# A selective-scan block with a quantised layer on one core: the quantised product formed transposed, its bias added by TensorE, and x1's statistics and x*D moved to ScalarE

## The chip, the cores and the metric

One core of one Trainium2 chip runs the whole kernel. The metric is the device time of one execution in microseconds (us). The kernel before took 2896.49 us (median of three runs, 2894.33 to 2896.74). The profile is of a further execution, which took 2897.0 us, of which 2895.2 us are the profiled span; the working of the prediction starts from that execution.

The five engines are called TensorE (PE in the profile; its weight loads are PEld), VectorE (DVE), ScalarE (ACT), GpSimd (POOL) and SyncE (SP, which issues most transfers). Each takes its instructions in the order in which the program lists them for it.

## The reference

x is 8 x 2048 tokens of 512 channels, float32. Cut to what matters:

```python
def layernorm(x):                     # over the 512 channels
    return (x - mean(x)) / sqrt(var(x) + 1e-5)

u     = layernorm(x)
xp    = u @ x_proj.T                  # 64 + 16 + 16 columns: d_rank, B, C
delta = softplus(d_rank @ dt_proj.T + dt_b)
# per channel d and state n (16 of them), over the 2048 tokens of a batch row:
h[t]  = exp(delta[t] * A) * h[t-1] + delta[t] * B[t] * u[t]
y[t]  = sum_n h[t] * C[t] + u[t] * D
x1    = x + y

z     = layernorm(x1)
scale = max(max|z|, 1e-6) / 127       # one per token
q     = clip(round(z / scale), -128, 127)
out   = x1 + (q @ wq.T) * scale * w_scale + bias
```

## The kernel before

**Tiling.** The 16,384 tokens are cut into 32 chunks of 512 (`k`). A chunk has four channel tiles of 128 (`d`) and 16 states, that is 64 scans of 128 channels x 512 tokens. One scan is one VectorE instruction (`scan`, L828). The program is written out as a sequence of 64 **slots** to a chunk, one scan each (L1105 to L1128). Four slots make a group `s`: two states by two channel tiles. Groups 0 to 7 of a chunk are channel pair `dp` 0 (slots 0 to 31), groups 8 to 15 are `dp` 1 (slots 32 to 63).

**What a scan needs.** ScalarE makes its factor exp(delta*A) (`exp_unit`, L766, tile `da`, three buffers of a group each). TensorE makes its second input delta*B*u in PSUM (`b_pe`, L813, tile `pb`, two buffers): one call of 8 products, recorded as 16 matmuls, serves two scans, and is issued at every even slot `u` for scans `u+2` and `u+3`. So the products of slot `u` can't start before scan `u-1` has freed their buffer. GpSimd multiplies each finished group with C (`c_mult`, L855) and, except in the first chunk of a batch row, writes the carried first column of `da` (`carry`, L780). TensorE then turns the products back and adds them up in PSUM (`y_pe`, L888, tile `y`, one buffer): 16 transposes 10 slots and 16 more 12 slots after the group's first slot.

**Beside the scans** two stages are spread over the slots by tables (L27 to L82). `prep(k)` makes the next chunk ready: statistics (L248, L252), normalisation (L310), four turned tiles (L322, L328), `xp` (L334, L344), four products `pdt` (L365), four softplus (L375), and four products delta*u (`dlt_pe` L288, `du` L388). `post(k)` runs one chunk later and finishes a chunk: `residual` copies x1 out of PSUM (L619), statistics of x1 on VectorE, `norm` (L633), `amax` (L652), `scales` and `inverses`, `add_bias` on GpSimd (L645), `rnd` (L670), four transposes each in `q_pe` (L675), `q_act` (L681), `o_pe` (L692), `o_out` (L701, VectorE) and `add_x1` on GpSimd (L713). The last two chunks use `LATE_AT`.

**What sets the order.** `keep_in_program_order` pins every instruction, so the tables are the order. In a slot the exps come first, then `b_pe` and the scan, then what the tables put there. Exps run ahead of the scans by up to 11 (L96, L1116 to L1119), but none is issued in the slots of `EXP_NONE`, around the softplus, because exp and softplus take a table load (ACT_TABLE_LOAD) at each change between them. The tiles of `misc` (L283, two PSUM buffers) are used in turn by `pxn`, `pxp`, `pbt`, `pdt`, `pdl`, `pz` and `po`.

**Start.** `prep_first` prepares chunk 0; `zero_diagonals` and `store_diagonals` (L214, L268) fill a table in DRAM from which `load_dg` (L799) fetches the diagonal matrices of B. All those transfers are in SP's queue.

Of the kernel before, what the change touches and what calls it, by code (L numbers as in the profile page):

```python
# [17 lines left out]
P = 128  # L18
# [10 lines left out]
    aggregate=(-49, -49, -44, -39),  # L29
    rstd=-37,  # L30
    norm=(-1, 0, 1, 2),
    xnt_pe=(4, 4, 8, 8),
    xnt_act=(6, 6, 10, 10),
    xp_pe=(10, 12, 16, 18),
    xp_act=20,
    bt_pe=22,
    bt_act=23,
    dt_pe=(24, 26, 30, 32),
    softplus=(27, 28, 32, 34),
    carry_mul=36,  # L40
    carry_exp=44,
    dlt_pe=(38, 38, 42, 42),
    du=(40, 41, 43, 44),
# [3 lines left out]
    residual=(9, 10),  # L47
    stats=(13, 16, 18, 22),
    aggregate=(19, 21, 24, 25),
    rstd=26,  # L50
    norm=(35, 36, 37, 38),
    amax=(38, 41),
    scales=42,
    inverses=45,
    add_bias=(40, 44),
    rnd=(46, 47, 48, 49),
    q_pe=(50, 50, 58, 60),
    q_act=(52, 53, 60, 62),
    o_pe=(54, 56, 62, 64),
    o_out=(56, 58, 64, 66),  # L60
    add_x1=(60, 68),
    store=(66, 74),
# [3 lines left out]
    residual=(9, 10),  # L66
    stats=(14, 18, 20, 20),
    aggregate=(18, 19, 20, 21),
    rstd=21,
    norm=(24, 25, 27, 30),  # L70
    amax=(28, 31),
    scales=32,
    inverses=34,
    add_bias=(33, 36),
    rnd=(37, 39, 39, 43),
    q_pe=(38, 42, 46, 50),
    q_act=(41, 43, 47, 51),
    o_pe=(44, 48, 52, 54),
    o_out=(46, 50, 54, 56),
    add_x1=(55, 60),  # L80
    store=(60, 64),
# [5 lines left out]
REUSED = 3  # L87
LOAD_AT = (18, 20)
SKIP_AT = ((20, 20, 22, 28), (48, 48, 52, 52))
ADD_X_AT = ((34, 36), (66, 70))  # L90
LAST_ADD_X_AT = (58, 60)
FIRST_HALF_AT = (41, 42)
Y_AT = (10, 12)
Y_FIRST_AT = (12, 14)
EXP_NONE = (27, 28, 29, 30, 31, 32, 33)
# [4 lines left out]
def kernel(  # L100
# [38 lines left out]
    bcp = ctx.enter_context(tc.tile_pool(name="bc", bufs=5))  # L139
# [48 lines left out]
    pin(nc.sync.dma_start(out=dsk_sb, in_=d_skip.rearrange("(c p) -> p c", p=P)))  # L188
    for k in range(1, min(3, NCHUNK)):
        load_x(k)  # L190
    wq_i32 = work.tile([P, ND, OUT // 4], I32, tag="hc", bufs=3, name="wq_i32")
    pin(nc.sync.dma_start(out=wq_i32, in_=wq_t.rearrange("(c p) o -> p c o", p=P)))
    zeros = work.tile([P, T], F32, tag="hc", bufs=3, name="zeros")
    pin(nc.vector.memset(zeros, 0.0))
# [5 lines left out]
    diag_d = const.tile([P, ND, P], F32, name="diag_d")  # L200
    wq_sb = const.tile([P, ND, OUT], BF16, name="wq_sb")
    ws_b = const.tile([P, OUT], F32, name="ws_b")
    bias_b = const.tile([P, OUT], F32, name="bias_b")
# [22 lines left out]
    def gpsimd_constants():  # L226

        for d in range(ND):
            pin(
                nc.gpsimd.tensor_scalar(  # L230
                    diag_d[:, d, :], ident, dsk_sb[:, d : d + 1], None, ALU.mult
                )
            )
        pin(nc.gpsimd.tensor_copy(wq_sb, wq_i32.bitcast(I8)))

# [5 lines left out]
    mvs, nmrs, rstds, x1, zs, qts = {}, {}, {}, {}, {}, {}  # L241
    das, pbs, dgs, hs, hcs, ys = {}, {}, {}, {}, {}, {}

    def stats(key, i, src):
        if key not in mvs:
            mvs[key] = small.tile([P, 2 * NT, 2], F32, tag="mv", bufs=2, name=f"mv_{key}")
        st = small.tile([P, 6], F32, tag="st", name=f"st_{key}_{i}")
        pin(nc.vector.bn_stats(st, src))  # L248
        sts[key, i] = st
# [4 lines left out]
    def rstd_of(key, first, n):  # L254

        mv = mvs.pop(key)[:, ds(first, n), :]
        ve = small.tile([P, n], F32, tag="ve", name=f"ve_{key}")
        pin(nc.gpsimd.tensor_scalar(ve, mv[:, :, 1], LN_EPS, None, ALU.add))
        rstd = small.tile([P, n], F32, tag="rstd", name=f"rstd_{key}")
        pin(nc.gpsimd.tensor_tensor(rstd, ve, nhalf[:, :n], ALU.pow))  # L260
        nm = small.tile([P, n], F32, tag="nm", name=f"nm_{key}")
        pin(nc.gpsimd.tensor_scalar(nm, mv[:, :, 0], -1.0, None, ALU.mult))
        nmr = small.tile([P, n], F32, tag="nmr", name=f"nmr_{key}")
        pin(nc.gpsimd.tensor_tensor(nmr, nm, rstd, ALU.mult))  # L264
        for i in range(n):
            nmrs[key, first + i], rstds[key, first + i] = nmr[:, i : i + 1], rstd[:, i : i + 1]
# [35 lines left out]
    def prep(k):  # L302
# [98 lines left out]
        def carry_exp():  # L401
# [4 lines left out]
            stats=lambda i: stats(key, NT + i, xn[k][:, i, :]),  # L406
            aggregate=lambda i: aggregate(key, NT + i),
# [7 lines left out]
            du=du,  # L415
        )
# [4 lines left out]
        if k in (1, 2):  # L421
            once["rstd"] = lambda: rstd_of(key, NT, NT)
# [8 lines left out]
    def prep_first(second):  # L431
# [161 lines left out]
        pin(nc.sync.dma_start(out=ws_b, in_=w_scale.partition_broadcast(P)))  # L593
        pin(nc.sync.dma_start(out=bias_b, in_=bias.partition_broadcast(P)))
# [22 lines left out]
    def residual(k, dp, half):  # L617
        t = x1[k].rearrange("p i (d h c) -> p i d h c", h=2, c=HALF)[:, :, ds(2 * dp, 2), half, :]
        pin(nc.scalar.copy(t, ys[k, dp][:, half, :, :, :]))  # L619

    def post(k):
# [7 lines left out]
        def norm(i):  # L629
            if i == 0:  # L630
                zs[k] = work.tile([P, NT, DM], F32, tag="z", bufs=1, name=f"z_{k}")
            pin(
                nc.scalar.activation(  # L633
                    zs[k][:, i, :],
                    x1_of(i),
                    AF.Identity,
                    bias=nmrs.pop((key, i)),
                    scale=rstds.pop((key, i)),
                )
            )  # L640

        def add_bias(j):
            t = x1[k][:, ds(2 * j, 2), :]
            b = bias_b.unsqueeze(1).to_broadcast([P, 2, OUT])
            pin(nc.gpsimd.tensor_tensor(t, t, b, ALU.add))  # L645

        def amax(j):
            if j == 0:
                st["am"] = small.tile([P, NT], F32, tag="am", name=f"am_{k}")
            two = slice(2 * j, 2 * j + 2)  # L650
            pin(
                nc.vector.tensor_reduce(  # L652
                    st["am"][:, two], zs[k][:, two, :], AX.X, ALU.max, apply_absolute_value=True
                )
            )
# [11 lines left out]
        def rnd(i):  # L667

            z = zs[k][:, i, :]
            pin(nc.scalar.activation(z, z, AF.Copy, bias=ROUND, scale=st["rs"][:, i : i + 1]))  # L670

        def q_pe(i):
            pz = misc(f"pz_{k}_{i}")
            for d in range(ND):
                pin(nc.tensor.transpose(pz[:, ts(d, P)], zs[k][:, i, ts(d, P)], ident))  # L675
            st["pz", i] = pz

        def q_act(i):
            qt = work.tile([P, ND, P], BF16, tag="qT", name=f"qT_{k}_{i}")
            pin(  # L680
                nc.scalar.activation(  # L681
                    qt, st.pop(("pz", i)).rearrange("p (d t) -> p d t", t=P), AF.Copy, bias=-ROUND
                )
            )
            qts[i] = qt

        def o_pe(i):
            po = misc(f"po_{k}_{i}")
            qt = qts.pop(i)
            for d in range(ND):  # L690
                pin(
                    nc.tensor.matmul(  # L692
                        po, lhsT=qt[:, d, :], rhs=wq_sb[:, d, :], start=(d == 0), stop=(d == ND - 1)
                    )
                )
            st["po", i] = po

        def o_out(i):

            pin(  # L700
                nc.vector.scalar_tensor_tensor(  # L701
                    zs[k][:, i, :],
                    st.pop(("po", i)),
                    st["xs"][:, i : i + 1],
                    ws_b,
                    ALU.mult,
                    ALU.mult,
                )
            )

        def add_x1(j):
            o = zs[k][:, ds(2 * j, 2), :]
            pin(nc.gpsimd.tensor_tensor(o, o, x1[k][:, ds(2 * j, 2), :], ALU.add))  # L713

        def store(j):
# [3 lines left out]
                    in_=zs[k][:, ds(2 * j, 2), :],  # L719
# [6 lines left out]
            residual=lambda half: residual(k, DP - 1, half),  # L726
            stats=lambda i: stats(key, i, x1_of(i)),
            aggregate=lambda i: aggregate(key, i),
# [4 lines left out]
            o_pe=o_pe,  # L733
            o_out=o_out,
        )
        pair = dict(amax=amax, add_bias=add_bias, add_x1=add_x1, store=store)
        n = 2 * NT if k + 3 < NCHUNK else NT
        once = dict(rstd=lambda: rstd_of(key, 0, n), scales=scales, inverses=inverses)
# [160 lines left out]
    def skip_pe(k, dp, i):  # L899

        for d2 in range(2):
            d = 2 * dp + d2
            for half in range(2):
# [5 lines left out]
                        rhs=diag_d[rows, d, rows],  # L909
# [5 lines left out]

    def finish():


        k, s = NCHUNK - 1, LAST - 1
        dp, np_ = place(s)[1:]  # L920
# [77 lines left out]
        def turned(i):  # L998
            qt = work.tile([P, ND, P], BF16, tag="qT", name=f"qT_last_{i}")
# [79 lines left out]
    for s in range(LAST - 1):  # L1079
        for part in range(2):  # L1080
            at = (Y_AT if s % NPAIR else Y_FIRST_AT)[part]
            plan(4 * s, [(at, lambda s=s, part=part: y_pe(s, part))])
    for k in range(NCHUNK):
        plan(k * SLOTS, [(LOAD_AT[j], lambda k=k, j=j: load_x1(k, j)) for j in range(2)])
        for dp in range(DP):
# [6 lines left out]
        plan(  # L1092
            k * SLOTS,
            [(FIRST_HALF_AT[h], lambda k=k, h=h: residual(k, 0, h)) for h in range(2)],
        )
# [82 lines left out]
```

## Time and profile before

| | us |
|---|---|
| three runs | 2894.33, 2896.49, 2896.74 |
| the profiled execution | 2897.0 |
| its span | 2895.2 |
| DVE busy, share | 2714.7, 94% |
| POOL busy, share | 2762.3, 95% |
| PE busy, share | 2577.8, 89% |
| ACT busy, share | 2061.6, 71% |
| bn statistics (L248) 244 times, 672 ns each | 158.8 |
| add_bias (L645) 62 times, add_x1 (L713) 62 times | 146.5, 147.3 |

How to read it: a group's line has the line of the kernel, the engine, the operation, output <- inputs, their sizes and the count; then busy time in all and the mean of one in ns; then the idle time of that engine just before these instructions and what ended most of it. The mean of one includes the part that overlaps with the next instruction: two scans in a row take 2.33, six 6.85, so one more scan costs 1.12 or so. A busy share is a mean over all stages. In the waits view a line says which instruction waited for which, the total in us, how many times, and the longest.

### The profile page before, as it was taken

How to read it: one execution, taken by the hardware profiler on the slowest of the kernel's cores; microseconds unless marked ns; L12 is line 12 of the kernel's file. 1: busy time of each engine (PE TensorE's matmuls, PEld its weight loads, DVE VectorE, ACT ScalarE, POOL GpSimd, SP SyncE). 2: the span in 40 equal slices, each digit the busy share in tenths (PEclk: the TensorE clock that was granted, in tenths of full speed). 3: DMA queues.
4: the chain of work that ended last, by engine and by line, in shares of the span. 5: the costliest groups of instructions: out<-in, count | busy, mean ns of one | idle time of the engine just before them, and what ended most of it. 6: DMA issues, size and time to landing. Idle time of an engine off the chain costs nothing.

```text
span 2895.2 us, 89048 instructions
## 1 busy us (share of the span) xinstructions
PE 2577.8 (89%) x37880; PEld 2077.8 (72%) x37880; DVE 2714.7 (94%) x2950; ACT 2061.6 (71%) x3550; POOL 2762.3 (95%) x1238
## 2 busy tenths in 40 slices
PE   7888998988988889989899998999998998998977
PEld 6777776766776777777777777777777777776766
DVE  5999999999999999999999999999999999999998
ACT  5777767777677776777776786767777767777764
POOL 4999999999999999999999999999999999999998
PEclk8999999999999999999999999999999999999998
DMA  6545455455554555554555445555545555555551
GB/s 199 148 126 155 162 162 171 132 139 164 166 165 137 140 155 166 157 165 131 144 165 167 162 142 139 155 165 157 158 137 147 166 166 163 143 137 154 145 168 63
DMA packets 298091, 440.24 MB, mean 152 GB/s; under 512 B 150944, under 2 KB 151456, under 8 KB 293728
## 3 DMA queue, kind: packets, MB, share of 16 engines
q1 hardware_dynamic: 296640, 434.32, 50.9%
q8 instruction: 300, 4.92, 0.7%
q14 instruction: 95, 0.78, 0.1%
q10 hardware_dynamic: 1056, 0.23, 0.0%
HBM read 394.63 MB, written 39.85 MB: 150 GB/s over the span
## 4 chain that ended last, share of the span: by engine, by line
DVE 42%; PE 30%; ACT 14%; issue 8%; DMA 4%; POOL 2%; SPq 0%; DVEq 0%; ACTq 0%; POOLq 0%
DVE h L828 34%; PE pb L813 13%; ACT da L766 6%; PE y L888 6%; PE y L906 3%; PE pdt L365 3%; ACT L766 3%; DMA dg<-dg 3%; DVE st L248 3%; DVE z L701 2%; POOL hc L855 2%; DVE x L388 1%; ACT z L633 1%; ACT L375 1%; DVE am L652 1%
## 5 line engine op out<-in xcount | busy, mean ns | idle before, releaser
L828 DVE TENSOR_TENSOR_SCAN h<-da,pb 128x512 f32<-128x512 f32 x2048 | 2348.5, 1200 | 85.4 <-PE pb L813 44.0
L855 POOL TENSOR_TENSOR hc<-h,c 128x2048 f32<-128x2048 f32 x511 | 2320.9, 4548 | 41.9 <-DVE h L828 21.7
L766 ACT ACTIVATE da<-delta,a_neg 128x511 f32<-128x511 f32 (+1 forms) x2048 | 1332.6, 712 | 529.3 <-DVE h L828 294.9
L813 PEld LDWEIGHTS pb<-dg,x 64*128 64x128 f32 x16384 | 1037.3, 192 | 697.1 <-issue 606.3
L813 PE MATMUL pb<-dg,x 64*128 64x128 f32 x16384 | 1218.6, 289 | 293.8 <-DVE h L828 143.4
L888 PE MATMUL y<-ident,hc 64*128 64x64 f32 x16352 | 688.9, 224 | 9.5 <-POOL hc L855 4.9
L888 PEld LDWEIGHTS y<-ident,hc 64*128 64x128 f32 x16352 | 658.4, 141 | 13.7 <-POOL hc L855 6.5
L375 ACT ACTIVATE delta<-pdt,dtb_sb 128x512 f32<-128x512 f32 x124 | 85.2, 687 | 157.0 <-PE pdt L365 156.3
L248 DVE BATCH_NORM_STATS2 st<-x 128x6 f32<-128x512 f32 x244 | 158.8, 672 | 0.0
L713 POOL TENSOR_TENSOR z<-z,x 128x1024 f32<-128x1024 f32 x62 | 147.3, 2376 | 0.0
L645 POOL TENSOR_TENSOR x<-x,bias_b 128x1024 f32<-128x1024 f32 x62 | 146.5, 2362 | 0.1
L601 PE MATMUL y<-x,ident 128*128 128x512 f32 x256 | 144.8, 648 | 0.0
L906 PE MATMUL y<-diag_d,xnT 64*128 64x64 f32 x2048 | 143.6, 272 | 0.0
L365 PE MATMUL pdt<-xp,dtproj_sb 128*128 128x512 f32 x248 | 140.5, 649 | 0.0
L334 PE MATMUL pxp<-xnT,xproj_sb 128*96 128x512 f32 x248 | 137.2, 635 | 0.0
L906 PEld LDWEIGHTS y<-diag_d,xnT 64*128 64x128 f32 x2048 | 130.8, 189 | 0.8 <-issue 0.8
L652 DVE TENSOR_REDUCE am<-z 128x2 f32<-128x1024 f32 x62 | 74.8, 1207 | 60.2 <-ACT z L633 60.2
L692 PE MATMUL po<-wq_sb,qT 128*128 128x512 bf16 x496 | 128.6, 382 | 0.0
L780 POOL TENSOR_TENSOR da<-first_a,state 128x4 f32<-128x4 f32 x384 | 82.6, 215 | 40.6 <-DVE h L828 35.6
L670 ACT ACTIVATE z<-z,rs 128x512 f32<-128x512 f32 x124 | 85.4, 712 | 24.7 <-DVE rs L664 24.7
L633 ACT ACTIVATE z<-x,nmr,rstd 128x512 f32<-128x512 f32 x124 | 99.0, 800 | 3.5 <-POOL nmr L264 3.5
L310 ACT ACTIVATE x<-x,nmr,rstd 128x512 f32<-128x512 f32 x120 | 95.6, 804 | 0.0
(108 smaller groups left out, 1523.8 us busy)
## 6 DMA issues: line engine op xcount, KB each, us to landing
c<-bc SPq DMA_DIRECT2D x416, 512.0 KB, 4.4
dg<-dg SPq DMA_DIRECT2D x413, 256.0 KB, 4.8
x<-in_x_dram SPq DMA_DIRECT2D x64, 512.0 KB, 6.3
x<-in_x_dram SPq DMA_DIRECT2D x31, 1024.0 KB, 6.3
out_dram<-z SPq DMA_DIRECT2D x62, 512.0 KB, 3.2
dg<-zeros SPq DMA_DIRECT2D x16, 256.0 KB, 6.6
x<-in_x_dram SPq DMA_DIRECT2D x4, 256.0 KB, 4.6
bc<-xp SPq DMA_DIRECT2D x32, 32.0 KB, 1.6
```

Of the source, the lines that this page charges most:

```text
L248: pin(nc.vector.bn_stats(st, src))
L334: nc.tensor.matmul(st["pp"][:E], lhsT=xproj_sb[:, d, :], rhs=xn_t[k][:, d, :], start=(d == 0), stop=(d == ND - 1),)
L365: nc.tensor.matmul(pd, lhsT=dtproj_sb[:, ts(d, P)], rhs=xp, start=True, stop=True)
L601: nc.tensor.matmul(ys[k, dp][:, half, :, :, :], lhsT=ident, rhs=t, start=False, stop=False, skip_group_check=True,)
L645: pin(nc.gpsimd.tensor_tensor(t, t, b, ALU.add))
L713: pin(nc.gpsimd.tensor_tensor(o, o, x1[k][:, ds(2 * j, 2), :], ALU.add))
L766: nc.scalar.activation(das[s][:, n2, d2, own], delta[k][:, d, own], AF.Exp, scale=a_neg[:, d, n : n + 1])
L813: nc.tensor.matmul(pb[:, h, :, i, :], lhsT=xn[k][rows, i, ts(d, P)], rhs=dgs[k, np_][rows, i, :, :], start=True, stop=True,)
L828: nc.vector.tensor_tensor_scan(hs[s][:, n2, d2, :], das[s][:, n2, d2, :], pbs[u // 2].rearrange("p h q i n -> p (h q i) n")[:, :, n2], 0.0 ...
L855: nc.gpsimd.tensor_tensor(hc, h, c.unsqueeze(2).to_broadcast([P, 2, 2, T]), ALU.mult)
L888: nc.tensor.matmul(ys[k, dp][:, half, i, d2, :], lhsT=hc[rows, ts(i, P)], rhs=ident[rows, rows], is_transpose=True, start=first, stop=last ...
L906: nc.tensor.matmul(ys[k, dp][:, half, i, d2, :], lhsT=xn_t[k][rows, d, ts(i, P)], rhs=diag_d[rows, d, rows], start=False, stop=False, skip ...
```

## The change

`post` and what surrounds it are rebuilt:

- x1 leaves PSUM by `y_out`, four ScalarE instructions of 256 columns for each `dp`, which also sum each token's row. GpSimd adds the two sums. Four ScalarE `square` instructions give the variance. VectorE's `stats` and `aggregate` of x1 go; those of x stay.
- After `y_out` has read `y`, TensorE adds the bias into the same PSUM tile (`bias_pe`, two bf16 matmuls with three rows, the bias split into three bf16 parts). `xb_act` then copies x1 + bias into a tile `xb`. `add_bias` and `add_x1` on GpSimd go.
- `norm` and `rnd` work in place on x1. `o_pe` has the weights stationary and all 512 tokens moving, so the product comes out with channels on partitions; `u_act` scales it by w_scale (one per partition) on ScalarE; `ut_pe` turns it back with four transposes per 128 tokens; `o_out` multiplies by the token's scale and adds `xb` in one VectorE instruction.
- x*D is multiplied by ScalarE in place (`skip_act`, once `xp` has been made), and `skip_pe` becomes plain transposes.
- Slots move. `dt_pe` goes from (24, 26, 30, 32) to (26, 28, 32, 34), the softplus from (27, 28, 32, 34) to (28, 29, 33, 35), `EXP_NONE` from 27-33 to 28-34, `amax` from (38, 41) to (28, 30), `rnd` from 46-49 to 37-40, `q_pe` from (50, 50, 58, 60) to (42, 42, 50, 50). `y`'s first transposes go from slots 12 and 14 of a `dp` to slot 14.
- `bc` has 4 buffers where it had 5, and 2 groups of a chunk where it was 3 reuse the C and diagonals of the first half.
- At the start GpSimd splits the bias (three casts, two copies, two subtractions, one partition of 512) where it made `diag_d`; the three transfers of the parts stand in SP's queue ahead of `zero_diagonals(0)`. The two broadcasts of w_scale and bias go from there to slot 20 of the last chunk.

```diff
 PREP_AT = dict(
-    dt_pe=(24, 26, 30, 32),
-    softplus=(27, 28, 32, 34),
+    dt_pe=(26, 28, 32, 34),
+    softplus=(28, 29, 33, 35),
+    skip_act=(30, 30, 31, 31),
-    dlt_pe=(38, 38, 42, 42),
-    du=(40, 41, 43, 44),
+    dlt_pe=(40, 40, 44, 44),
+    du=(42, 43, 45, 46),
...
 POST_AT = dict(
+    sums=11,
+    squares=(14, 15, 16, 17),
+    rstd=22,
+    norm=(25, 26, 26, 27),
+    amax=(28, 30),
+    scales=31,
+    inverses=36,
+    rnd=(37, 38, 39, 40),
+    q_pe=(42, 42, 50, 50),
+    q_act=(44, 45, 52, 53),
+    o_pe=(54, 56, 58, 60),
+    u_act=(56, 58, 60, 62),
+    ut_pe=(64, 64, 66, 66),
+    o_out=(66, 67, 68, 69),
+    store=(72, 76),
...
-FIRST_HALF_AT = (41, 42)
+Y_OUT_AT = ((41, 41, 42, 42), (73, 73, 74, 74))
+BIAS_AT = (43, 75)
+XB_AT = ((44, 45), (76, 77))
-Y_FIRST_AT = (12, 14)
+Y_FIRST_AT = (14, 14)
-EXP_NONE = (27, 28, 29, 30, 31, 32, 33)
+EXP_NONE = (28, 29, 30, 31, 32, 33, 34)
...
+    def y_out(k, dp, i):
+            nc.scalar.activation(
+                x1[k][:, i, ds(dp * 2 * P, 2 * P)].rearrange(...),
+                ys[k, dp][:, :, i, :, :].rearrange("p h d c -> p d h c"),
+                AF.Identity,
+                accum_out=x1[k, "s"][:, dp, i : i + 1],
...
+    def bias_pe(k, dp):
+        for half in range(2):
+                nc.tensor.matmul(
+                    ys[k, dp][:, half, :, :, :],
+                    lhsT=ones_3,
+                    rhs=row[:, :, half, :].unsqueeze(1).to_broadcast([3, NT, 2, HALF]),
+                    start=False, stop=False, skip_group_check=True,
...
+    def skip_act(k, d):
+        t = xn_t[k][:, d, :]
+        pin(nc.scalar.activation(t, t, AF.Copy, scale=dsk_sb[:, d : d + 1]))
```

The two queues of the changed kernel, as built, between slots 24 and 50 of a chunk ("wait" names what the built program waits for there):

```
ScalarE: exp 32,33; xp; exp 34,35; norm x1 0; BT; state; norm 1,2,3; table load;
  softplus 0,1; state; skip_act x4; softplus 2; state; table load; exp 36,37;
  table load; softplus 3; table load; exp 38,39; exp 40,41; rnd 0; state; exp 42,43;
  rnd 1; exp 44,45; rnd 2; exp 46,47; rnd 3; exp 48,49; y_out x2; state; exp 50,51;
  y_out x2; exp 52,53; q_act 0; xb 0; exp 54,55; q_act 1; xb 1; ...
TensorE: slot 32: b_pe (wait: scan 31), y x16, pdt 2; slot 34: b_pe, y x16, pdt 3; ...
  slot 42: b_pe, pz 0, pz 1, bias x2 (wait: the fourth y_out);
  slot 44: b_pe for scans 46, 47; pdl 2 (wait: q_act 0); pdl 3 (wait: du 2);
  slot 46: b_pe for scans 48, 49; y of the next dp (wait: xb 1); ...
VectorE: ...; scan 44; scan 45; du 2; scan 46; du 3; scan 47; ...
```

## The prediction

> **What bounds the kernel now.** I began with the costliest groups of the page, to see which engine has least air.
>
> ```profile
> L828 DVE TENSOR_TENSOR_SCAN h<-da,pb 128x512 f32<-128x512 f32 x2048 | 2348.5, 1200 | 85.4 <-PE pb L813 44.0
> L855 POOL TENSOR_TENSOR hc<-h,c 128x2048 f32<-128x2048 f32 x511 | 2320.9, 4548 | 41.9 <-DVE h L828 21.7
> ```
>
> VectorE and GpSimd are both about 95% busy, so the shares don't say who leads. The waits of VectorE between the first and the last amax (182 to 2820 us) do:
>
> ```profile
> DVE am L652 <- ACT z L633: 60.2, 31, 2.2
> DVE h L828 <- ACT da L766: 32.6, 26, 1.3
> DVE h L828 <- PE pb L813: 27.7, 44, 2.5
> DVE h L828 <- POOL hc L855: 2.3, 3, 1.0
> ```
>
> VectorE hardly waits for GpSimd: 2.3 us in 30 chunks. It waits for ScalarE and TensorE. So VectorE leads: a chunk's amax waits end at 1421.04 and 1773.54, four chunks apart, 88.1 us each. Of that VectorE's work is 64 scans of 1.12, 8 statistics of 0.59, 8 aggregates of 0.07, two amax of 1.11, four du of 0.60, four o_out of 0.65, together 84.3 (starts of neighbours on its timeline). The other 3.8 are waits, all in one place. VectorE's timeline there:
>
> ```profile
> 1407.04 6.85 DVE L828 TENSOR_TENSOR_SCAN h<-da,pb 128x512 f32<-128x512 f32 x6 [0.29 <-PE pb L813]
> 1414.23 2.33 DVE L828 TENSOR_TENSOR_SCAN h<-da,pb 128x512 f32<-128x512 f32 x2 [0.34 <-PE pb L813]
> 1417.79 1.22 DVE L828 TENSOR_TENSOR_SCAN h<-da,pb 128x512 f32<-128x512 f32 x1 [1.23 <-ACT da L766]
> 1421.04 1.22 DVE L652 TENSOR_REDUCE am<-z 128x2 f32<-128x1024 f32 x1 [2.03 <-ACT z L633]
> ```
>
> These are scans 30-35, 36-37, 38 and the first amax. ScalarE's timeline at the same time shows why:
>
> ```profile
> 1410.39 0.69 ACT L375 ACTIVATE delta<-pdt,dtb_sb 128x512 f32<-128x512 f32 x1 [3.83 <-PE pdt L365]
> 1411.10 1.28 ACT L766 ACT_TABLE_LOAD   x1
> 1412.39 1.33 ACT L766 ACTIVATE da<-delta,a_neg 128x511 f32<-128x511 f32 x2
> 1413.74 1.28 ACT L375 ACT_TABLE_LOAD   x1
> 1415.04 0.69 ACT L375 ACTIVATE delta<-pdt,dtb_sb 128x512 f32<-128x512 f32 x1
> 1415.74 1.28 ACT L766 ACT_TABLE_LOAD   x1
> 1417.04 1.33 ACT L766 ACTIVATE da<-delta,a_neg 128x511 f32<-128x511 f32 x2
> ...
> 1428.44 1.04 ACT L619 COPY x<-y 128x512 f32<-128x512 f32 x2
> ```
>
> From the third softplus, which waits for TensorE, ScalarE works without a gap; scan 38 starts as soon as its exp is there. The windows view confirms it for 1410.39 to 1429.48, with its columns PE, PEld, DVE, ACT, POOL:
>
> ```profile
> 1410.39:1429.48 19.09, 15.81 (x198) 12.79 (x198) 15.50 (x16) 19.00 (x27) 16.10 (x8) 0.91 0.21 64
> ```
>
> ScalarE is busy 19.00 of 19.09 us, in the stage where the change adds most to it.
>
> **The sum, part by part.**
>
> *VectorE loses* four statistics and four aggregates of x1: 4 x 0.59 + 4 x 0.07 = 2.65 a chunk; 81.65 of work stay. o_out is one instruction as before (another second input; 0.65).
>
> *GpSimd loses* four instructions of 2.35 and gains about 0.7 of small ones. I count both at nothing: by the waits, VectorE doesn't wait for it. *TensorE* loses half the passes of x*D (L906's 16 in 0.89 become transposes like L888's 16 in 0.49) and gains 16 transposes (8 in 1.02, L675) and four bias matmuls: even in sum, but moved.
>
> *First stall.* The third product pdt is now at slot 32 behind the `b_pe` that waits for scan 31, so it can't be earlier than the end of scan 31. Its chain stands in the trace before one pdt earlier (1403.05 to 1405.87): wait 0.07, `b_pe` 1.16, y 0.49, pdt 1.05, then softplus; 2.85. From the softplus to scan 38 the trace has 1410.39 to 1417.79, 7.4; a state copy (0.1) is added between. So scan 38 starts 10.35 after scan 31 has ended; six scans and the reciprocal need 6.8. **3.55 lost**, where before 3.8 were lost between the late exps and amax. Amax itself no longer waits: by its slots 28 and 30 its two norms are done (rstd ends 7.8 after scan 19, two norms and BT 1.7 more: 9.5; VectorE gets there at 10.1). The four `skip_act` (0.61 each, as L670) fall into ScalarE's wait for pdt 2, about 2.1 long after them.
>
> Three table loads stand in that chain, 1.29 each from start to start. The Trainium skill (ScalarE: Activation LUTs, "What ACT_TABLE_LOAD costs") gives about 2.66 us for a switch with its drain; by that the chain, and the stall, would be 4.1 longer, which the row of before excludes.
>
> *Second stall*, the step on which the forecast rests. Count from the start of scan 38. ScalarE then issues, in its built order, 13 exps, four `rnd`, two state copies, four `y_out`. Before, from 1417.79 to 1428.44, it did 13 exps and four norms of 0.70 in 10.65. With `rnd` at 0.61: -0.36; copies +0.2; `y_out` 4 x 0.40 = 1.6. The fourth `y_out` ends at 12.1. (The trace has no `y_out`. Nearest below: the last chunk's copy of the same size, L1031, four in 1.2, 0.30 each; above: that and another small ScalarE instruction for the sum, 0.19 as L866, and some slack, 0.60. I take 0.40, near the row of equal size.) Before, only y's first transposes at slot 44 waited for this copy, after the `b_pe` of their slot. Now the bias waits for it on TensorE, and behind it stand `b_pe` for scans 46-47, pdl 2, pdl 3, `b_pe` for 48-49.
> - Bias: two bf16 matmuls, 0.49 (L692: four in 0.98; from half that to the two passes of L601, 1.05). `b_pe` 1.1: at 13.8.
> - pdl 2 waits for q_act 0 as well, two exps and 0.58 later: 12.1 + 1.8 = 13.9; transposes 0.6; VectorE's du 2 at 14.7 to 15.35.
> - pdl 3 waits for du 2; `b_pe` for 48-49 ends at 17.2. Scan 46 from 15.35, du 3, scan 47; scan 48 at 18.2.
> - Needed: ten scans and four du, 13.6. **4.6 lost** (3.8 to 6 by the bounds).
>
> *Third*: four pairs of slots in a row (54 to 60) now have `b_pe`, y and po on TensorE: 2.55 each (1444.86 to 1447.41) against 2.24 for two scans, in a stretch from which o_out has gone; 1.25 less a lead of about 0.6: **0.7 lost** (0 to 1.2).
>
> *Other additions*, counted at nothing: `square`, `u_act`, `xb_act` (0.71, 0.5, 0.5, after L633, L681, L619) lie in slots where ScalarE had slack (44.78 us busy of the 68.88 from 1429.48 to 1498.36, in the windows view). If that cover went, they would cost their 7 us. The same bias order at slot 11 leaves about 0.1 before scan 14; each 0.1 on `y_out` there costs up to 0.4. One more C and one more diagonal load a chunk: the diagonals of group 15 stand on SP behind a C load that waits for group 11's `c_mult`; by 4.8 to land they come 0.5 ahead of need; about 1 if not.
>
> A chunk: 81.65 + 3.55 + 4.6 + 0.7 = 90.5 against 88.1: **+2.4**, times 30 full chunks = 72. First chunk, with neither rounding nor q_act: both stalls smaller, +3.5. Last chunk: statistics only, -2.65. Start: SP's zero fills, issued at 26.72 before, stand behind bias parts that GpSimd has only after 29.9 and seven small instructions, 3.3 to 8.9 (a quarter of L234's cast to L1053's 1.27, each seven times); 6.5 to 12 later, two broadcasts fewer; scan 12 waited for these fills' successors (9.32): +6. Sum: +79, on the profiled 2897.0, that is 2976; the median of the runs is 0.5 lower: **2975**.
>
> The Trainium skill (Perfetto Trace Analysis, "Optimizing Scalar/DVE Operations") says that offloading to ScalarE may make sense where VectorE is saturated. By the shares of the page (94% and 71%) it holds, and would give 31 x 2.65 = 82 us; by ScalarE's 19.00 of 19.09 in this stage it doesn't.
>
> **The rivals.**
> - *VectorE keeps what it saves* (faster). Work falls by 2.65 and the old waits stay: 2897 - 82 + 6 = 2821. It is decided at slot 43: du 2 is wanted 10.2 after scan 38, and needs the fourth `y_out` at 7.6. For: the averages. Against: 13 exps alone take 8.0. Chance 0.09.
> - *GpSimd was the limit* and its 9.4 go straight to the time, down to VectorE's 81.65 a chunk: 2897 - 31 x 6.45 + 6 = 2703. For: 95% busy. Against: 2.3 us of waits. 0.03.
> - *The change moves work but the loss only balances it*: the second stall 2.2, not 4.6; 2903. Needs ScalarE some 2.4 ahead of my count. 0.05.
> - *More is late*: `y_out` at 0.60 also delays slot 12 (+0.8 twice), TensorE's run 1.2, the diagonals 1: +2.3 a chunk more, 3045. 0.11.
>
> **How the numbers follow.** The forecast has 0.72: 2975, its own range 2925 to 3020. A difference under 0.2% (6 us) can't be told from none. Faster is the first two rivals, 0.12; same 0.05; slower 0.83. The range runs from 2905, the balance, to 3030, part of the last rival; it leaves out about 0.17.
>
> **What would show it.** In the profile after: VectorE's wait for `pb` and for pdl once a chunk, some 4.6 together, about 15 us after the third softplus; TensorE idle before the bias until a `y_out`; waits for `da` twice, 1.2 and 2.3; no wait before amax; GpSimd well under 90%. The forecast is wrong if `b_pe` at slot 44 isn't late, or if the two `da` waits are gone.

## The result, and the profile after

The changed kernel takes 3011.36 us (median of four runs, 3009.24 to 3013.56), the kernel before 2896.61 beside it: ratio 1.0397, 95% interval 1.0379 to 1.0415. It is slower by 115 us; 2975 was forecast, 79 more. Its profiled span is 3009.0, 113.8 more than before.

The groups of the page of the changed kernel, which answer to those shown of before (the scan is now L913, GpSimd's product L940):

```profile
L913 DVE TENSOR_TENSOR_SCAN h<-da,pb 128x512 f32<-128x512 f32 x2048 | 2351.6, 1200 | 172.4 <-ACT da L851 109.1
L940 POOL TENSOR_TENSOR hc<-h,c 128x2048 f32<-128x2048 f32 x511 | 2320.6, 4546 | 157.2 <-PE y L973 64.4
L413 DVE TENSOR_TENSOR x<-pdl,x 128x512 f32<-128x512 f32 x124 | 84.2, 679 | 159.6 <-PE pdl L313 157.8
L658 PE MATMUL y<-bias,ones 3*128 3x512 bf16 x124 | 38.0, 386 | 91.7 <-ACT x L646 91.7
```

The scans cost what they did; the idle time ahead of them doubled (85.4 to 172.4), and du (L413), which did not wait before, has 159.6 of idle time ahead of it, 157.8 of that for the transposes pdl (`dlt_pe`). The bias on TensorE (L658) waits 91.7 for ScalarE's y_out (L646). GpSimd is 83% busy and waits too. VectorE's waits in the same stretch as before, 182 to 2820 us:

```profile
DVE x L413 <- PE pdl L313: 150.2, 44, 6.0
DVE h L913 <- ACT da L851: 101.9, 58, 2.2
DVE h L913 <- PE pb L898: 32.3, 98, 1.2
DVE h L913 <- POOL da L865: 3.0, 8, 0.4
```

The waits of amax are gone, as forecast. In their place stand du's wait, once a chunk, and the exps', twice a chunk (58 in 29 chunks). VectorE's timeline has them all in one stretch of a chunk (scan 36, scan 38 and on, du 0, du 2, scan 48):

```profile
1563.26 1.22 DVE L913 TENSOR_TENSOR_SCAN h<-da,pb 128x512 f32<-128x512 f32 x1 [1.33 <-ACT da L851]
...
1567.85 5.89 DVE L913 TENSOR_TENSOR_SCAN h<-da,pb 128x512 f32<-128x512 f32 x5 [2.20 <-ACT da L851]
1574.16 0.69 DVE L413 TENSOR_TENSOR x<-pdl,x 128x512 f32<-128x512 f32 x1 [0.42 <-PE pdl L313]
...
1583.49 0.69 DVE L413 TENSOR_TENSOR x<-pdl,x 128x512 f32<-128x512 f32 x1 [4.70 <-PE pdl L313]
...
1587.53 2.33 DVE L913 TENSOR_TENSOR_SCAN h<-da,pb 128x512 f32<-128x512 f32 x2 [0.30 <-PE pb L898]
```

From scan 38 at 1567.85 to du 2 at 1583.49 are 15.6 us, where 10.2 would do (eight scans of 1.12 and two du of 0.60). ScalarE's timeline (third softplus, the exps from 38 on, the second half of the fourth y_out, q_act 0) and its busy time from that softplus to the end of y_out, with the columns as before, show the queue behind it:

```profile
1560.38 0.69 ACT L400 ACTIVATE delta<-pdt,dtb_sb 128x512 f32<-128x512 f32 x1 [2.39 <-PE pdt L390]
...
1567.10 2.56 ACT L851 ACTIVATE da<-delta,a_neg 128x512 f32<-128x512 f32 x4
...
1579.67 0.20 ACT L646 ACTIVATION_READ_ACCUMULATOR x<-y 128x1 f32 x1
...
1580.99 0.59 ACT L752 ACTIVATE qT<-pz 128x512 bf16<-128x512 f32 x1
```

```profile
1560.38:1579.76 19.38, 14.54 (x166) 11.26 (x167) 14.36 (x15) 19.30 (x36) 15.64 (x5) 0.91 0.37 122
```

ScalarE is busy 19.30 of 19.38 us, and the exp behind the last y_out starts 11.9 after scan 38 did; for the end of y_out 12.1 was forecast. TensorE's timeline then shows what waits for it, and something that was not forecast:

```profile
1574.53 1.16 PE L898 MATMUL pb<-dg,x 64*128 64x128 f32 x16
...
1579.92 0.59 PE L658 MATMUL y<-bias,ones 3*128 3x512 bf16 x2 [2.59 <-ACT x L646]
1580.44 1.96 PE L898 MATMUL pb<-dg,x 64*128 64x128 f32 x16
1582.33 1.13 PE L313 MATMUL pdl<-ident,delta 128*128 128x128 f32 x4
...
1585.30 2.08 PE L898 MATMUL pb<-dg,x 64*128 64x128 f32 x16
```

The same 16 products of b_pe take 1.16 before the wait for y_out and 1.96 and 2.08 after it. The windows view, cut at the trace's own changes of the granted clock (the column after the five engines; 1.00 is full speed), shows with what it goes together:

```profile
1566.96:1570.37 3.41, 1.54 (x19) 0.68 (x15) 2.52 (x3) 3.40 (x8) 0.96 (x3) 1.00 0.43 141
1570.37:1573.78 3.41, 3.41 (x35) 3.29 (x36) 3.26 (x3) 3.41 (x6) 3.41 (x1) 0.50 0.27 97
...
1580.61:1587.44 6.83, 6.04 (x46) 5.09 (x48) 3.63 (x4) 4.05 (x10) 0.12 (x1) 0.50 0.39 115
```

In this chunk, after a stretch in which TensorE was busy 1.54 of 3.41 us, its clock is 0.50 for the next 3.41; after the wait for y_out it is 0.50 for another 6.83, just when everything late is queued on TensorE. That the clock is what costs there is tested below, by filling the wait.

**Where the 113.8 us are**, taken from the starts of the scans in the two traces: the start and chunk 0 +4.9, chunks 1 to 30 +117.3, the last chunk and the end -8.4. A chunk is from here on the mean of chunks 2 to 29, first scan to first scan:

| us a chunk | before | forecast for after | after |
|---|---|---|---|
| VectorE's work and gaps under 0.15 | 84.4 | 81.65 | 82.5 |
| waits at scans 36 and 38 (first stall) | 1.7 | 3.55 | 3.5 |
| wait of amax | 2.0 | 0 | 0 |
| waits from du 0 to scan 50 (second stall) | 0 | 4.6 | 5.7 |
| other waits | 0.4 | 0.7 | 0.7 |
| chunk | 88.5 | 90.5 | 92.4 |

### The profile page after: what moved, and what is told of

Same layout as the page of the kernel before. It is cut to its first block, busy times and chain, and to the rows that moved or that the text cites. A ratio compares the mean times of both kernels' runs of the same rounds, so it can differ in the third digit from the quotient of the medians.

```text
span 3009.0 us, 89095 instructions
## 1 busy us (share of the span) xinstructions
PE 2641.9 (88%) x37476; PEld 2082.4 (69%) x37476; DVE 2645.3 (88%) x2702; ACT 2391.1 (79%) x4552; POOL 2502.0 (83%) x1207
## 4 chain that ended last, share of the span: by engine, by line
PE 54%; ACT 24%; DVE 16%; issue 5%; DMA 1%; POOL 0%; SPq 0%; DVEq 0%; ACTq 0%; POOLq 0%
PE pb L898 23%; PE y L973 11%; ACT da L851 11%; DVE h L913 11%; PE pxp L359 4%; PE po L764 4%; ACT x L646 3%; PE pdt L390 3%; ACT L851 3%; DVE xb L791 2%; ACT x L740 2%; PE pdl L313 2%; ACT L400 1%; DVE am L722 1%; ACT delta L400 1%
## 5 line engine op out<-in xcount | busy, mean ns | idle before, releaser
L913 DVE TENSOR_TENSOR_SCAN h<-da,pb 128x512 f32<-128x512 f32 x2048 | 2351.6, 1200 | 172.4 <-ACT da L851 109.1
L940 POOL TENSOR_TENSOR hc<-h,c 128x2048 f32<-128x2048 f32 x511 | 2320.6, 4546 | 157.2 <-PE y L973 64.4
L898 PE MATMUL pb<-dg,x 64*128 64x128 f32 x16384 | 1239.5, 293 | 160.9 <-DVE h L913 103.1
L413 DVE TENSOR_TENSOR x<-pdl,x 128x512 f32<-128x512 f32 x124 | 84.2, 679 | 159.6 <-PE pdl L313 157.8
L400 ACT ACTIVATE delta<-pdt,dtb_sb 128x512 f32<-128x512 f32 x124 | 85.2, 687 | 91.4 <-PE pdt L390 90.5
L313 PE MATMUL pdl<-ident,delta 128*128 128x128 f32 x512 | 113.1, 372 | 24.6 <-DVE x L413 23.5
L764 PE MATMUL po<-qT,wq_sb 128*128 128x512 bf16 x496 | 128.6, 382 | 1.0 <-ACT qT L752 1.0
L658 PE MATMUL y<-bias,ones 3*128 3x512 bf16 x124 | 38.0, 386 | 91.7 <-ACT x L646 91.7
L313 PEld LDWEIGHTS pdl<-ident,delta 128*128 128x128 f32 x512 | 83.9, 214 | 46.9 <-DVE x L413 35.5
L708 ACT ACTIVATE x<-x,nmr,rstd 128x512 f32<-128x512 f32 x124 | 94.3, 808 | 15.0 <-POOL nmr L288 15.0
L784 PE MATMUL pu<-ident,x 128*128 128x128 f32 x496 | 74.7, 283 | 29.4 <-DVE xb L791 29.3
L776 ACT ACTIVATE x<-po,ws_col 128x512 f32<-128x512 f32 x124 | 83.9, 677 | 15.7 <-PE po L764 15.7
L335 ACT ACTIVATE x<-x,nmr,rstd 128x512 f32<-128x512 f32 x120 | 94.9, 804 | 0.0
L740 ACT ACTIVATE x<-x,rs 128x512 f32<-128x512 f32 x124 | 87.4, 707 | 5.9 <-DVE rs L734 5.9
```

What stands on the lines that cost most here:

```text
L313: nc.tensor.matmul(out, lhsT=turned_tokens(src, i), rhs=ident[:n, :n], is_transpose=True, start=True, stop=True,)
L400: nc.scalar.activation(delta[k][:, d, :], st.pop(("pd", d)), AF.Softplus, bias=dtb_sb[:, d : d + 1])
L764: nc.tensor.matmul(po, lhsT=wq_sb[:, d, ts(o, P)], rhs=qts[k][:, d, :], start=(d == 0), stop=(d == ND - 1),)
L898: nc.tensor.matmul(pb[:, h, :, i, :], lhsT=xn[k][rows, i, ts(d, P)], rhs=dgs[k, np_][rows, i, :, :], start=True, stop=True,)
L913: nc.vector.tensor_tensor_scan(hs[s][:, n2, d2, :], das[s][:, n2, d2, :], pbs[u // 2].rearrange("p h q i n -> p (h q i) n")[:, :, n2], 0.0 ...
L940: nc.gpsimd.tensor_tensor(hc, h, c.unsqueeze(2).to_broadcast([P, 2, 2, T]), ALU.mult)
```

## The experiments

My theory is the prediction's: two stalls, each the end of a queue. The first is the softplus chain, whose third product stands behind a `b_pe` that waits for scan 31. The second is TensorE's, which waits for y_out and q_act at the end of ScalarE's queue while `b_pe` and pdl stand behind. New in it is the clock: what is late then runs at half speed. Rivals: one sum of work (ScalarE's, TensorE's or GpSimd's) is the limit, and the order only says where it shows; or the bias itself is the cost.

| run | us, median | ratio to before, 95% | chunk, us | at half clock, us a chunk |
|---|---|---|---|---|
| after | 3011.4 | 1.0397 (1.0379 to 1.0415) | 92.4 | 8.0 |
| fewer exps ahead | 2892.2 | 0.9994 (0.9985 to 1.0004) | 88.6 | 3.9 |
| pdt earlier | 2928.1 | 1.0116 (1.0097 to 1.0135) | 89.7 | 6.6 |
| both | 2809.9 | 0.971 (0.9694 to 0.9726) | 85.9 | 0.9 |
| no bias | 3004.4 | 1.0382 (1.0367 to 1.0398) | 92.2 | 9.5 |
| wait filled | 2969.6 | 1.0257 (1.0242 to 1.0272) | 91.1 | 2.7 |
| no bias, wait filled | 2982.8 | 1.03 (1.0283 to 1.0318) | 91.4 | 4.6 |
| squares twice | 3010.8 | 1.0406 (1.0389 to 1.0423) | 92.1 | 7.0 |
| before, without GpSimd's adds | 2883.9 | 0.9963 (0.995 to 0.9976) | 88.6 | 4.0 |
| before, without x1's statistics | 2840.8 | 0.9815 (0.9801 to 0.983) | 86.6 | 3.7 |
| both, and q_act earlier | 2791.3 | 0.964 (0.9625 to 0.9654) | 85.3 | 1.1 |
| and softplus 2, 3 together | 2752.5 | 0.9512 (0.9497 to 0.9526) | 84.1 | 0.5 |
| and pdl 2 earlier | 2744.2 | 0.948 (0.9464 to 0.9496) | 83.8 | 0.7 |

The last column is from the mean granted clock of chunks 2 to 29: for the changed kernel 0.9565, so 2 x 0.0435 x 92.4 = 8.0; the kernel before has 3.4. The ratio is to the kernel before as it ran beside each run.

**Fewer exps ahead in slots 36 to 42.**

```diff
-            if slot not in EXP_NONE and ahead < min((s + 3) * 4, u + EXP_AHEAD):
+            far = 4 if 36 <= slot <= 42 else EXP_AHEAD
+            if slot not in EXP_NONE and ahead < min((s + 3) * 4, u + far):
```

> The changed kernel, with exps at most 4 scans ahead in slots 36 to 42 (11 before), nothing else. Theory (the second stall is the bias waiting for y_out at the end of ScalarE's queue): six exps fewer stand ahead of the fourth y_out, 6 x 0.63 = 3.8, so it ends 8.1 after scan 38 and not 11.9; q_act 0 ends at about 11.1, du 2 at 11.8 and not 15.6 (wanted at 10.2), scan 48 at about 14.8 and not 19.3. The wait at du 2 falls from 5.0 to about 1.5 a chunk, the time by about 4 x 30 = 120, to 2890 (2865 to 2915). Rival (ScalarE's or TensorE's work in sum, or GpSimd, sets the chunk, and the order within a queue only says where the wait is seen): the wait goes to another place, 3011 within 15. Second rival: exps so late that scans 43 to 50 wait for da: waits for da there, 3000 or more.

Measured: 2892.2, 119 less, for exactly the same instructions in another order. VectorE's two largest waits between 182 and 2550 us:

```profile
DVE h L913 <- ACT da L851: 93.4, 53, 2.2
DVE x L413 <- PE pdl L313: 47.3, 40, 2.3
```

The waits for the exps stay, du's falls from 5.2 a chunk to 1.8 (1.6 of it at du 2). The order within ScalarE's queue made the second stall, not the sum of its work. With this one edit the changed kernel takes as long as the kernel before.

**The third and fourth pdt one pair of slots earlier.**

```diff
-    dt_pe=(26, 28, 32, 34),
+    dt_pe=(26, 28, 30, 32),
```

> The changed kernel with the third and fourth product pdt at slots 30 and 32 (32 and 34 in it), nothing else. Theory (the first stall is the softplus chain, gated by a product that stands behind the b_pe that waits for scan 31): the third pdt comes some 2.3 earlier and the third softplus follows the four x*D directly; the two waits for da, 1.3 and 2.2 a chunk, fall to about 0 and 1.2: 2.3 x 31 = 71 less, 2940 (2925 to 2960). Rival (TensorE has no room before slot 32: the two products then make b_pe late, and scans 32 to 35 wait for pb instead): 3011 within 15.

Measured: 2928.1, 83 less. The same two waits, in the same stretch:

```profile
DVE x L413 <- PE pdl L313: 156.2, 27, 6.0
DVE h L913 <- ACT da L851: 28.6, 27, 1.1
```

The wait at scan 36 is gone and that at scan 38 is 1.06, as expected, and no new wait for pb appeared. Du 2's wait grew from 4.9 to 5.8 a chunk while the small ones beside it went: the second stall as a whole is as large as it was (5.8 for 5.7).

**Both edits.**

> Both edits: exps at most 4 ahead in slots 36 to 42, and the third and fourth pdt at slots 30 and 32. Theory (two stalls, each with its own cause, one after the other): the gains add, 4 + 2.3 a chunk, 3011 - 190 = 2820 (2795 to 2850), and a chunk takes about 86 us, of which 82.6 is VectorE's work. Rival (one limit behind both, so that what the one gives the other takes): no better than the better of the two alone, about 2890.

Measured: 2809.9, 201 less where the two alone gave 119 and 83. They add, as expected: the stalls have separate causes. TensorE then has 0.9 us a chunk at half clock.

**Without the bias matmuls** (the call of `bias_pe` taken out).

> The changed kernel without its two bias matmuls per half chunk (the bias is left out of the output), nothing else. Theory (what is late is ScalarE: pdl 2 waits for q_act 0, which stands behind y_out in ScalarE's queue, so the matmuls themselves are little): b_pe for scans 46 and 47 is on time, but du 2 still comes about 0.7 after q_act 0, at 14.3 and not 15.6 after scan 38: 1 to 2 less a chunk, 2950 to 2980. Rival (the wait of the bias is all of the second stall): 5.4 x 30 less, 2850.

Measured: 3004.4, 7 less: neither. TensorE in the place of the bias's wait:

```profile
1576.62 1.16 PE L898 MATMUL pb<-dg,x 64*128 64x128 f32 x16
1580.99 1.13 PE L313 MATMUL pdl<-ident,delta 128*128 128x128 f32 x4 [3.20 <-ACT qT L752]
...
1583.96 2.08 PE L898 MATMUL pb<-dg,x 64*128 64x128 f32 x16
```

`b_pe` for scans 46 and 47 is on time, but pdl 2 waits for q_act 0, a little behind y_out in the same queue. TensorE idles 3.2 in place of 2.6, and is 9.5 us a chunk at half clock in place of 8.0. Du 2's wait falls by 0.8, and the waits just before and after it grow by 0.4. The rival that the bias is the cost falls; my number (2950 to 2980) fell too. I had left the clock out of it, which a run below shows to be a part of the miss.

**The wait filled with work.**

```diff
+        if dp == 0 and k > 0:
+            for _ in range(5):
+                for d in range(ND):
+                    pin(nc.tensor.transpose(pz_1[k - 1][:, ts(d, P)], x1[k - 1][:, 1, ts(d, P)], ident))
```

> The changed kernel; ahead of the bias of the first half, TensorE repeats the four transposes of pz 1 five times over into the same tile (20 in all, about 2.6 us), so that it works where it waits for y_out. Theory (the second stall came out 1 to 1.5 a chunk longer than forecast because TensorE, after its 2.6 us of waiting, runs what is late at half clock: b_pe 2.08 in place of 1.16): b_pe for scans 46 and 47 takes 1.2 again, the granted clock after the bias is 1.0, and the time falls by 1 to 1.5 a chunk, 2965 to 2985. Rival (the clock costs nothing that counts; the stall was sized wrongly for ScalarE's queue): 3011 within 8, or longer by what the transposes delay q_act 1.

Measured: 2969.6, 42 less, by adding 20 transposes a chunk. TensorE's timeline:

```profile
1467.48 2.35 PE L659 MATMUL pz<-ident,x 128*128 128x128 f32 x20
1470.03 0.59 PE L666 MATMUL y<-bias,ones 3*128 3x512 bf16 x2 [0.20 <-ACT x L646]
1470.55 1.16 PE L908 MATMUL pb<-dg,x 64*128 64x128 f32 x16
```

`b_pe` takes 1.16 again, and pdl 2, which follows, 0.75 in place of 1.13. The waits from du 0 to scan 50 are 4.6 a chunk, the number that was forecast at full clock, where they were 5.7. So the clock is the 1.1 a chunk by which the second stall was longer than forecast; the chunk is shorter by 1.4 in all.

**Without the bias, and filled** (the same transposes, no bias matmuls).

> The kernel without the bias matmuls (left out of the output), with the 20 repeated transposes of pz 1 in their place at slot 43, as in the run that filled the wait. Without the bias TensorE had waited 3.2 us for q_act 0 ahead of pdl 2 (2.6 for y_out before) and then run pdl 2, pdl 3 and b_pe at half clock (1.13, 1.13 and 2.08 us). Theory (what the bias gave back, the clock took): with the wait filled these take 0.6, 0.6 and 1.16, and the time is 1.2 to 1.9 a chunk shorter than without the bias, 3004 - 36 to 57 = 2945 to 2970; it is also below the run that keeps the bias and fills (2970). Rival (pdl 2's wait for q_act 0 is all there is, whatever the clock): 3004 within 8.

Measured: 2982.8, 22 less than without the bias. The direction is the theory's, the size about half (22 for 36 to 57), and it isn't below the filled run with the bias, but 13 above. Du 2 waits 4.1 in both, so without the bias too it is q_act 0 that sets it. Here 4.6 us a chunk stay at half clock against 2.7, with 1.52 still idle ahead of pdl 2; whether that is all of the 13 was not tried. It stays above the 2950 to 2980 that I had expected without the bias, so the clock doesn't account for all of that miss; the rest is open.

**Each square done twice** (a second step `again` of the same squares, in the same slots).

> The changed kernel with each of the four squares of a chunk done twice (the second overwrites the first with the same), 4 x 0.72 = 2.9 us more for ScalarE in slots 14 to 17. Theory (squares lie in slack, the loss is in two places of the queue): 3011 within 10. Rival (ScalarE's work in sum is the limit): 31 x 2.9 = 90 longer, 3100.

Measured: 3010.8. 2.9 us more of ScalarE's work a chunk cost nothing. ScalarE's sum is not the limit; squares lie in slack, as the prediction counted them.

**The kernel before without GpSimd's two adds** (`add_bias` and `add_x1` out of its list of steps).

> The kernel before without GpSimd's add_bias and add_x1 (the bias and x1 are left out of the output): GpSimd has 9.4 us less to do in each chunk. Theory (VectorE hardly waits for GpSimd): as the kernel before, 2897 within 10. Rival (GpSimd, 95% busy, is the limit): up to 31 x 6.4 = 200 shorter, 2700.

Measured: 2883.9, 11 less than the kernel before beside it and a little more than the 10 allowed for; a chunk is unchanged (88.6). What it gains is at the end: the last chunk and what follows take 105.9, where the kernel before takes 115.2. GpSimd was no limit but there.

**The kernel before without x1's statistics** (`stats` and `aggregate` of x1 out of its steps, chunks 0 to 28).

> The kernel before without VectorE's statistics of x1 in chunks 0 to 28 (x1 is normalised with the statistics of the x of a later chunk, so the output is another): VectorE loses the 2.65 a chunk that the change takes from it, and nothing is put in their place. Theory (VectorE leads outside one stage): most of 29 x 2.65 = 77 goes from the time, 2820 to 2840; the waits around slots 36 to 39 stay about 3.5 a chunk. Rival (ScalarE's and TensorE's chain sets the chunk already in the kernel before): the waits grow by what the work falls, 2890 to 2897.

Measured: 2840.8, 54 less, just past the upper end of what was expected. VectorE's work falls by 2.3 a chunk, the waits grow by 0.5 (scan 28 waits 0.7 in place of 0.3, scan 36 now 0.2 for GpSimd). So with the old slots 1.85 of the 2.65 a chunk that the change takes from VectorE come through where nothing is put on ScalarE and TensorE instead.

**Both edits, exps at most 3 ahead, q_act 0 and 1 one slot earlier.**

> Both edits that helped, with exps at most 3 ahead (4 before) in slots 36 to 42, and q_act 0 and 1 one slot earlier (43 and 44). Theory: one exp fewer stands before the fourth y_out and two fewer between it and q_act 0, 3 x 0.63 = 1.9; du 2's wait of 1.8 a chunk goes to 0 to 0.3 and leaves 0.35, 0.25 and 1.05 in the other places: about 1.6 x 30 = 48 less than with the two edits, 2760 (2750 to 2785). Rival (GpSimd is next: its c_mult is 4.5 for each of 16 groups, 72 of 85.9 a chunk, and its carry comes late): 2800 or more, with waits for POOL. Second rival (exps come late): waits for da at scans 43 to 47.

Measured: 2791.3, a gain of 19 and not 48. Du 2 still waits 1.2 a chunk: y_out ends early enough, but on TensorE pz 1 waits for du 1 to free its PSUM buffer, then bias, `b_pe` and pdl 2 follow in a row. No wait for GpSimd appeared.

**The fourth softplus straight after the third** (`dt_pe` (26, 28, 30, 31), `softplus` (28, 29, 33, 34)).

> The version before this one (2791), with the fourth product pdt at slot 31 (32) and the fourth softplus at slot 34 (35), so that all four products come before the b_pe that waits for scan 31, and no exp stands between the third and the fourth softplus: two table loads of 1.29 go. Theory (what is left of the first stall is those loads): exp 36 ends at 3.3 after the third softplus started, exp 38 at 4.6, where it was 7.4; the wait for da at scan 38, 1.05 a chunk, goes, and ScalarE is 2.6 earlier for rnd and y_out too, so that of du 2's 1.16 about half goes: 1.6 x 30 = 48 less, 2743 (2730 to 2765). Rival (TensorE has no room for both products ahead of slot 32): a new wait for pb at scans 34 to 36 of 1.05, no gain, 2791 within 10.

Measured: 2752.5, 39 less, in the expected range. The wait for exps is gone from VectorE's waits; two table loads of 1.28 were the rest of the first stall. Du 2's wait fell only from 1.2 to 0.9.

**Pdl 2 ahead of b_pe** (`dlt_pe` (40, 40, 43, 44)).

> The same, with pdl 2 one slot earlier (43), ahead of the b_pe for scans 46 and 47. Theory (after the first two mends, du 2 waits for TensorE alone: bias 0.55, b_pe 1.1, pdl 0.7 in a row): du 2 0.5 to 0.9 earlier, of which b_pe then takes 0.3 back: 0 to 20 less than the run beside it. Rival (pdl 2 waits for q_act 0 there and holds up b_pe): 5 to 30 longer than the run beside it.

Measured: 2744.2, 8 less, in the expected range. It is the best version: 5.2% below the kernel before, 8.8% below the changed one, with all of the change in it. A chunk is 83.8 us, 82.0 of it VectorE's work. VectorE's largest wait left is that of the scans for pb, 51.0 us between 182 and 2550 us, in 111 places.

## Why the prediction was right in direction and short in size

- **VectorE leads, GpSimd doesn't**: right. Taking 9.4 us a chunk from GpSimd leaves the chunk as it is; taking 2.65 from VectorE gives 1.85.
- **VectorE's saving**, 2.65 a chunk: 1.9 measured (84.4 to 82.5). Most of the difference is in small things: a scan that another follows at once takes 1.12 from start to start, one ahead of a wait 1.20, and after has 7.3 such scans a chunk, before 3.6 (0.3); gaps under 0.15 add 0.2. The rest I can't place.
- **First stall**: right, 3.5 for 3.55, at the places (1.3 and 2.2 for 1.2 and 2.3) and with the cause named; moving the product took 2.4 of it away. The waits of before were not quite "all in one place": of 4.1 a chunk, 0.4 stand at scans 28 and 30.
- **Second stall**: its mechanism right, its size short, 5.7 for 4.6. The queue on ScalarE was timed well (the queue is past the last y_out at 11.9 for 12.1; one y_out is 0.36 from start to start for 0.40). What failed is the price of what stands behind it on TensorE: `b_pe` 1.1 and pdl 0.6 came from rows at full clock. With the wait filled, the stall is 4.6. The sign could be read before: the prediction's own window of this stage has a granted clock of 0.91, and in it TensorE's timeline of the kernel before has the same 16 products at 2.08, behind a wait:

  ```profile
  1423.53 2.08 PE L813 MATMUL pb<-dg,x 64*128 64x128 f32 x16 [2.52 <-DVE h L828]
  ```

  The Trainium skill (TensorE: Matmul & The Clock Gate, "What's actually happening") has the two states, half and full clock, and free-running windows of 3.413 us; this trace agrees, in pieces of 3.41 and 6.83 at 0.50. Its rule of thumb ("HAM oscillation") is to leave no idle gap over about 3.4 us; here shorter waits were enough, of 1.9 us in most chunks and of 2.4 to 3.3 us in all (counted below), so the measurement goes further than the rule. The place given among the signs, "about 15 us after the third softplus", should have been after scan 38: du 2 came 15.6 after that scan and 23.1 after the softplus.
- **Third**, 0.7 in slots 54 to 60: no wait is there. 0.6 of the 0.7 a chunk of other waits are at scans 0 and 28 instead, and 0.3 at scan 28 stood there before; the sum came out by chance.
- **Counted at nothing**: right for the squares, by the doubled run; `u_act` and `xb_act` were not tried by themselves. TensorE waits for diagonals only twice, 13.3 us at the start and 2.3 in the last chunk, so the extra loads cost nothing in the chunks between.
- **Start and first chunk**, +9.5: +4.9. SP's zero fills came 9.5 later, as said (36.23 for 26.72), but scan 12 only 2.0 (62.53 for 60.57), in part because the fills were issued faster (4.40 for 5.84) and the two broadcasts no longer stood among them.
- **End**, -2.65: -8.4, of which 4.4 for a reason told below.
- **Sum**: the changed chunk came out 1.9 above the forecast (92.4 for 90.5): 0.8 VectorE's work, 1.1 the second stall, the rest as forecast in sum. The chunk of before was 88.5 and not 88.1 over so many chunks, so the difference is 3.9 for 2.4, 1.5 more in each of 30 chunks; the start and the end came out 10 better, which hides a part of it.
- The **rivals**: that VectorE keeps its saving failed at the place it was to be decided, the fourth y_out, past at 11.9 where 7.6 was needed. With y_out and the products earlier the saving comes through: the same change with other slots is 5.2% below the kernel before. What the kernel before would gain from such slots (its waits are 4.1 a chunk) was not tried. "More is late" was right in size, 3045 being as near as 2975, but not in its parts: y_out is short, and TensorE's run and the diagonals cost nothing that shows.

## What to carry to other kernels

When work is moved to an engine with a low average share, read how busy that engine is in the stage where it lands, and who waits in order behind its last instruction; running an engine far ahead (here exps 11 scans ahead) can itself delay whatever shares its queue. A wait of some 2 us on TensorE can cost more than its length: what is queued behind it can run at half clock, so price it from rows at that clock. And test a suspected wait by taking out what stands ahead of the releaser, not the waiting instruction: taking out the bias that waited gave 7 us, six exps fewer ahead of the y_out that it waited for gave 119.

## What the runs showed of the hardware

- TensorE's granted clock halves after waits shorter than 3.41 us. In chunks 2 to 29 of the changed kernel it was at half within 2.1 us of the end of the wait for y_out (2.4 to 3.3 us) in all 28 chunks, and after the wait ahead of `b_pe` some 10 us earlier (1.6 to 1.9 us) in 17 of 26; in the kernel before, after waits of 2.5 to 2.6 us ahead of `b_pe`, in 20 of 24. Where in the clock's own windows the wait lies seems to decide: all changes of the clock in these chunks fall on one grid of 3.413 us, and of the grid's windows at full clock those that a half-clock window followed had TensorE busy 0.05 to 0.59 of the time (45 windows), the others 0.50 or more (648). 20 useless transposes in the wait made the kernel 42 us shorter.
- An accumulated sum on ScalarE is an instruction of its own: ACTIVATION_READ_ACCUMULATOR, 0.196 us by itself and 0.09 to 0.10 from start to start; a y_out of 256 columns is 0.27 and that.
- VectorE's last product with C (four of 128 x 512, two operands in SBUF) took 6.86 us in the kernel before and 2.47 in the changed one. VectorE in the kernel before, then in the changed one:

```profile
2867.72 6.86 DVE L927 TENSOR_TENSOR hc_last<-h,c 128x512 f32<-128x512 f32 x4
```

```profile
2986.67 2.47 DVE L1022 TENSOR_TENSOR hc_last<-h,c 128x512 f32<-128x512 f32 x4
```

  GpSimd in the kernel before at that time:

```profile
2860.92 8.98 POOL L855 TENSOR_TENSOR hc<-h,c 128x2048 f32<-128x2048 f32 x2
2869.87 2.35 POOL L713 TENSOR_TENSOR z<-z,x 128x1024 f32<-128x1024 f32 x1
```

  The first of the four took 5.05 and ended 0.55 after GpSimd's add; in the changed kernel GpSimd had finished, and it took 0.68. Without GpSimd's adds it took 0.945, with GpSimd busy for the first 0.4, and again ended 0.55 after it. The Trainium skill (GPSIMD Engine Reference, "8. Key points") says that GpSimd shares its SBUF interfaces with VectorE, with contention for VectorE's instructions with two SBUF inputs; the runs agree and give a size: both times VectorE's instruction ended 0.55 after GpSimd's last, as if it had stood still until then. The scans, whose second input lies in PSUM, run beside GpSimd at 1.12 all along. The shorter product is 4.4 of the 8.4 us that the end got shorter.
